# A four-layer graph network on one core: the second linear layer of the edge stages in two half products, and the loading of weights and zeros moved into the sort loop

## The chip, the cores and the metric

The kernel runs on one core of a Trainium2 chip. The metric is the time of one execution on the device in microseconds (us). Runs of one kernel agree within some 0.2%.

## What is computed

The program takes 12500 nodes with 16 features and 412500 edges (sorted by target) with 8 features and a weight, and runs four graph layers, each behind a LayerNorm and a ReLU and with a residual. The change touches the third layer, an encode-process network with 64 features, cut here to its edge part:

```python
def _mlp(x, w0, b0, w1, b1):
    return jax.nn.silu(x @ w0 + b0) @ w1 + b1
def _ln(x, g, b):
    m = jnp.mean(x, axis=-1, keepdims=True)
    v = jnp.var(x, axis=-1, keepdims=True)
    return (x - m) * jax.lax.rsqrt(v + LN_EPS) * g + b

e = _ln(_mlp(edge_feat, edge_enc_w0, edge_enc_b0, edge_enc_w1, edge_enc_b1), edge_enc_g, edge_enc_beta)
for s in range(2):
    ce = jnp.concatenate([e, n[senders], n[receivers]], axis=-1)
    e = e + _ln(_mlp(ce, edge_blk_w0[s], edge_blk_b0[s], edge_blk_w1[s], edge_blk_b1[s]), ...)
    agg = jax.ops.segment_sum(e, receivers, num_segments=num_nodes)
    ...
```

The other layers gather node features along the edges, weight them and sum them per target (or, in the first, per source).

## The kernel before

All work is in f32 but for some selection matrices. The program is one sequence of stages on one core:

1. **Start-up** (0 to 179 us). Constants; some 110 small DMAs on SyncE's queue for the weights of all layers (`load_w`, `load_b`, `pair_diag`, `bias_rows`, `twice`), with a little VectorE work on them (centering, splitting biases into three bf16 parts, block-diagonal copies); a zero tile of 128 x 6336 and ten DMAs that fill the sums in DRAM with it (`prep`, L322 to L327); LayerNorm of the nodes (`relu_ln`, L733 on) and a table for the first layer; `window_starts` (L340 to L358), which finds where the edges of each window of 128 targets begin.
2. **Sort loop** (`sort_edges`, to 4634 us). 98 windows of 128 targets. Per window `keys`, `hot_cells`, `count`, `look_up` and `rank` work out on VectorE and TensorE a row for each of 4480 records, and `scatter` (L597) writes them with 35 indirect DMAs that GpSimd issues; `s_row` (L593) is the tile of rows. Windows further back are read again and take the first layer's messages (`gather`, `products`, `message`, `to_sources`, L641 to L675). The order on TensorE, VectorE, ScalarE (ACT) and SyncE is written out by hand, window stages of lags 0 to 5 in one round, 103 rounds. The tile `s_row` has three buffers and the record tile `rec` four; a load of the next record tile waits on SyncE for an earlier window's scatters.
3. **Edge encoder** (4653 to 6786 us), **layer 2** (to 8155 us), **first edge update** (8333 to 10856 us), **second edge update** (11061 to 13350 us), with node work between them, then two GCN passes to the end.

The edge encoder and both updates run the same loop, `over_pairs`: 49 pairs of windows, ten chunks `c` of up to four blocks of 128 edges in two halves (features of two edges side by side on 128 partitions, 64 features each). The order of the engines is written out by hand; `new` is the pair whose hidden layer is made, `old` the pair before, which is normalised and summed. Per chunk: `hidden` (TensorE: first linear layer; in the updates the products L1507 and L1514 with features and gathered tables, in the encoder L1409), `scale` (VectorE: LayerNorm's factor and selection matrices), `features` (TensorE turns the old chunk, L1254, and ACT or VectorE writes it), `output` (the second linear layer, `outs`), `activate` (ACT: silu, L1209), `to_targets` (TensorE: sums per target, L1273).

`outs` (L1211 on) makes the second linear layer of a chunk: a bias product of 512 columns in bf16 (L1216), then per block of 128 edges a product of the hidden features (128 x 128, the stationary operand) with a 128 x 128 matrix that holds the 64 x 64 weights twice on its diagonal (L1218; `w1x` has them crossed, for odd chunks of the updates). All go into one PSUM bank `po`; ACT reads it twice, for the squares (L1221) and the copy `y` (L1223), and VectorE sums the squares (L1224). PSUM has eight banks here: `usual` gives two to `pt` (turns), five to `po` (hidden layers, outputs and other sums), one to `pa` (sums per target).

Other lines that are used below: `sums` of the encoder's `Adding` (L806: products of a 128 x 128 matrix with 16 columns) and the small product of a bias with weights (L278 to L280).

Of the kernel before, what the change touches and what calls it, by code (L numbers as in the profile page):

```python
# [19 lines left out]
P = 128  # L20
# [27 lines left out]
def tile_gnn(ctx: ExitStack, tc: tile.TileContext, a: dict, out: bass.AP):  # L48
# [23 lines left out]
    usual = dict(pt=2, po=5, pa=1)  # L72
    summing = dict(pt=2, po=4, pa=2)

    def bank(tag):
        pool, bufs = now[0]
        return pool.tile([P, 512], F32, name=tag, bufs=bufs[tag])
# [53 lines left out]
    def pair_diag(name, src, centered):  # L131

        d = consts.tile([P, P], F32, name=name)
        two = consts.tile([P, 64], F32, name=name + "_2")
        v.memset(d, 0.0)
        sp.dma_start(two[0:64, :], src)
        sp.dma_start(two[64:128, :], src)
        if centered:
            center(two, 64)
        v.tensor_copy(d[0:64, 0:64], two[0:64, :])  # L140
        v.tensor_copy(d[64:128, 64:128], two[64:128, :])
        return d

    def bias_rows(name, src, centered):

        b = consts.tile([3, 64], F32, name=name + "_f")
        sp.dma_start(b, row_bc(src, 64, 3))
        if centered:
            center(b, 64)
        part = consts.tile([3, 3, 64], BF16, name=name + "_p")  # L150
        back = consts.tile([3, 64], F32, name=name + "_b")
        acc = consts.tile([3, 64], F32, name=name + "_a")
        for k in range(3):
            v.tensor_copy(part[:, k, :], b)
            v.tensor_copy(back, part[:, k, :])
            v.tensor_sub(b, b, back)
            if k == 0:
                v.tensor_scalar(acc, back, ident[0:3, 0:1], None, op0=ALU.mult)
            else:
                v.scalar_tensor_tensor(acc, back, ident[0:3, k:k + 1], acc, op0=ALU.mult, op1=ALU.add)  # L160
        r = consts.tile([P, 8, 64], BF16, name=name)
        v.memset(r, 0.0)
        v.tensor_copy(r[0:3], acc[:, None, :].to_broadcast([3, 8, 64]))
        return r.rearrange("p t f -> p (t f)")
# [27 lines left out]
    wml = load_w("wml", a["L0_gnn_W_msg_lin"], 16, 16)  # L192
    v.tensor_scalar(wml, wml, 0.25, None, op0=ALU.mult)
    wupd = load_w("wupd", a["L0_gnn_W_upd_tp"].rearrange("i h k -> i (h k)"), 16, 256)
    v.tensor_scalar(wupd, wupd, 1.0 / 16.0, None, op0=ALU.mult)
    wul = load_w("wul", a["L0_gnn_W_upd_lin"], 16, 16)
    v.tensor_scalar(wul, wul, 0.25, None, op0=ALU.mult)
    w1t = load_w("w1t", a["L1_w_iao"], 16, 128)
    w1c = consts.tile([P, 16], F32, name="w1c")
    for j in range(8):  # L200
        sp.dma_start(w1c[16 * j:16 * j + 16, :], a["L1_w_iao"][:, 16 * j:16 * j + 16])
    b1_l1 = load_b("b1_l1", a["L1_gnn_bias"], 16)

    p2 = "L2_gnn_"
    ne_w0 = load_w("ne_w0", a[p2 + "node_enc_w0"], 16, 64)
    ne_b0 = load_b("ne_b0", a[p2 + "node_enc_b0"], 64)
    ne_w1 = load_w("ne_w1", a[p2 + "node_enc_w1"], 64, 64)
    center(ne_w1, 64)
    ne_b1 = load_b("ne_b1", a[p2 + "node_enc_b1"], 64)
    center(ne_b1, 64)  # L210
    ne_g = load_b("ne_g", a[p2 + "node_enc_g"], 64)
    ne_be = load_b("ne_be", a[p2 + "node_enc_beta"], 64)

    ee_w0 = consts.tile([P, 8, 64], F32, name="ee_w0")
    v.memset(ee_w0, 0.0)
    for t in range(TS):
        sp.dma_start(ee_w0[8 * t:8 * t + 8, t % 8, :], a[p2 + "edge_enc_w0"])
    ee_w0 = ee_w0.rearrange("p t f -> p (t f)")

    ec_w0 = consts.tile([P, 8, 64], F32, name="ec_w0")  # L220
    v.memset(ec_w0, 0.0)
    for t in range(8):
        sp.dma_start(ec_w0[WORDS * t:WORDS * t + 8, t, :], a[p2 + "edge_enc_w0"])
        sp.dma_start(ec_w0[WORDS * t + W_ONE:WORDS * t + W_ONE + 1, t, :], row_bc(a[p2 + "edge_enc_b0"], 64, 1))
    ec_w0 = ec_w0.rearrange("p t f -> p (t f)")
    ee_b0 = bias_rows("ee_b0", a[p2 + "edge_enc_b0"], False)
    ee_w1 = pair_diag("ee_w1", a[p2 + "edge_enc_w1"], True)
    ee_b1 = bias_rows("ee_b1", a[p2 + "edge_enc_b1"], True)
    ee_g = load_b("ee_g", a[p2 + "edge_enc_g"], 64)
    ee_be = load_b("ee_be", a[p2 + "edge_enc_beta"], 64)  # L230
# [8 lines left out]
    ee_g2 = twice("ee_g2", a[p2 + "edge_enc_g"])  # L239
    ee_be2 = twice("ee_be2", a[p2 + "edge_enc_beta"])  # L240

    eb, nb = [], []
    for s in range(2):
        w0, f = a[p2 + "edge_blk_w0"][s], {}
        f["w0e"] = pair_diag(f"eb_w0e{s}", w0[0:64, :], False)
        f["w0sd"] = consts.tile([64, 128], F32, name=f"eb_w0sd{s}")
        sp.dma_start(f["w0sd"][:, 0:64], w0[64:128, :])
        sp.dma_start(f["w0sd"][:, 64:128], w0[128:192, :])
        f["b0"] = load_b(f"eb_b0{s}", a[p2 + "edge_blk_b0"][s], 64)
        f["w1"] = pair_diag(f"eb_w1{s}", a[p2 + "edge_blk_w1"][s], True)  # L250
        f["w1x"] = consts.tile([P, P], F32, name=f"eb_w1x{s}")
        v.memset(f["w1x"], 0.0)
        sp.dma_start(f["w1x"][0:64, 64:128], f["w1"][64:128, 64:128])
        sp.dma_start(f["w1x"][64:128, 0:64], f["w1"][0:64, 0:64])
        f["b1"] = bias_rows(f"eb_b1{s}", a[p2 + "edge_blk_b1"][s], True)
        f["g"] = load_b(f"eb_g{s}", a[p2 + "edge_blk_g"][s], 64)
        f["be"] = load_b(f"eb_be{s}", a[p2 + "edge_blk_beta"][s], 64)
        f["g2"] = twice(f"eb_g2{s}", a[p2 + "edge_blk_g"][s])
        eb.append(f)
        f = {}  # L260
        f["w0"] = load_w(f"nb_w0{s}", a[p2 + "node_blk_w0"][s], 128, 64)
        f["b0"] = load_b(f"nb_b0{s}", a[p2 + "node_blk_b0"][s], 64)
        f["w1"] = load_w(f"nb_w1{s}", a[p2 + "node_blk_w1"][s], 64, 64)
        center(f["w1"], 64)
        f["b1"] = load_b(f"nb_b1{s}", a[p2 + "node_blk_b1"][s], 64)
        center(f["b1"], 64)
        f["g"] = load_b(f"nb_g{s}", a[p2 + "node_blk_g"][s], 64)
        f["be"] = load_b(f"nb_be{s}", a[p2 + "node_blk_beta"][s], 64)
        nb.append(f)

    eb[0]["sum_be"], eb[1]["sum_be"] = consts.tile([P, 64], F32, name="sum_be"), eb[1]["be"]
    v.tensor_add(eb[0]["sum_be"], eb[0]["be"], ee_be)

    be0 = twice("eb_be2", a[p2 + "edge_blk_beta"][0])
    be_w0e = consts.tile([P, 64], F32, name="be_w0e")
    with banks(**usual):
        pb0 = bank("pa")
        pe.matmul(pb0[:, 0:64], lhsT=be0[0:64, :].to_broadcast([64, P]), rhs=eb[1]["w0e"][0:64, 0:64], start=True,  # L278
                  stop=True)
        v.tensor_copy(be_w0e, pb0[:, 0:64])  # L280
    dec_w0 = load_w("dec_w0", a[p2 + "dec_w0"], 64, 64)
    dec_b0 = load_b("dec_b0", a[p2 + "dec_b0"], 64)
    dec_w1 = load_w("dec_w1", a[p2 + "dec_w1"], 64, 16)
    dec_b1 = load_b("dec_b1", a[p2 + "dec_b1"], 16)
    gw1 = load_w("gw1", a["L3_w1_t"], 16, 32)
    gb1 = load_b("gb1", a["L3_gnn_b1"], 32)
    gw2 = load_w("gw2", a["L3_w2_t"], 32, 16)
    gb2 = load_b("gb2", a["L3_gnn_b2"], 16)
# [33 lines left out]
    sp.dma_start(X, a["x"].rearrange("(p c) d -> p c d", c=C))  # L322
    with tc.tile_pool(name="prep", bufs=1) as wk:
        zero = wk.tile([P, (C + 1) * 64], F32, name="zero")
        v.memset(zero, 0.0)
        for t in [*g_l0, g_l1, *g_l2, *g_gc, t_acc]:
            sp.dma_start(t.rearrange("(p c) d -> p (c d)", p=P), zero[:, :t.shape[0] // P * t.shape[1]])  # L327
# [7 lines left out]
    def window_starts(wk):  # L335
# [4 lines left out]
        sp.dma_start(di, a["dst"].rearrange("(p j) -> p j", p=P))  # L340
        v.tensor_single_scalar(di, di, 7, op=ALU.arith_shift_right)
# [24 lines left out]
    def sort_edges():  # L366


        with tc.tile_pool(name="ws", bufs=1) as wk:
            window_starts(wk)  # L370
        with tc.tile_pool(name="so1", bufs=1) as one, tc.tile_pool(name="so", bufs=2) as ed, \
# [38 lines left out]
            with tc.manual_schedule(engines={et.PE, et.DVE, et.Activation, et.SP}):  # L410
                ws = [Window(g, k, ed) for g in range(ND)]
                ws[0].load()
                for g in range(ND + LAG):
                    def at(lag):
                        return [ws[g - lag]] if 0 <= g - lag < ND else []
# [49 lines left out]
                    for w in at(LAG - 2):  # L465
                        w.slot_rows()
            ok = one.tile([1, 1], F32, name="ok")
# [707 lines left out]
    class Pair:  # L1175
# [5 lines left out]
        def __init__(self, m, ed):  # L1181
            self.m, self.ed, self.ft, self.hot, self.ys = m, ed, {}, {}, {}
# [23 lines left out]
        def silu(self, po, c):  # L1206
            n = self.blocks(c) * P
            self.hid = self.ed.tile([P, 4 * P], F32, name="hidn", bufs=3)
            sc.activation(self.hid[:, :n], po[:, :n], AF.Silu)  # L1209

        def outs(self, c, w1, b1):  # L1211
# [593 lines left out]
```

## Time and profile before

| | us |
|---|---|
| median of 11 runs | 15569.72 (15546.02 to 15581.85) |
| profiled execution | 15571.9, of it the span of instructions 15570.1 |
| start-up to the first sort key | 179.4 |
| first scatter to last scatter of the sort | 214.3 to 4572 |
| edge encoder, 49 pairs | 4653 to 6786 |
| first, second edge update, 49 pairs each | 8333 to 10856, 11061 to 13350 |

| engine | busy us (share of the span) |
|---|---|
| TensorE, products | 11479.6 (74%) |
| TensorE, weight loads | 9472.5 (61%), beside the products |
| VectorE | 12500.1 (80%) |
| ACT | 6075.3 (39%) |
| GpSimd | 7104.4 (46%) |

The shares are means over stages with different bounds, so a stage has to be read by itself. PE is TensorE, PEld its weight loads, DVE VectorE, ACT ScalarE, POOL GpSimd, SP SyncE; a line number is one of the kernel. The durations of matmuls are partly modelled and overlap; what one costs is read from the start of one to the start of the next.

### The profile page before, as it was taken

What the parts mean: (1) busy time and instruction counts of PE and PEld (TensorE: products, weight loads), DVE (VectorE), ACT (ScalarE), POOL (GpSimd) and SP (SyncE); (2) the same over time, 40 slices, a digit from 0 to 9 for tenths busy, and PEclk for the clock granted to TensorE, in tenths of its full rate; (3) what the DMA queues carried; (4) which work ended last, traced back from release to release, by engine and by line L of the source; (5) the groups of instructions that cost most, each with busy time, mean ns of one, the idle gap of its engine ahead of it and who ended that gap; (6) DMA issues with size and microseconds to landing.
All of it is one profiled execution on the core that took longest, in us unless ns stands there. A gap on an engine that the chain in (4) does not pass through costs nothing. (4 is left out here: it accounts for less than half of the span.)

```text
span 15570.1 us, 386432 instructions
## 1 busy us (share of the span) xinstructions
PE 11479.6 (74%) x160695; PEld 9472.5 (61%) x161327; DVE 12500.1 (80%) x23622; ACT 6075.3 (39%) x10025; POOL 7104.4 (46%) x6387
## 2 busy tenths in 40 slices
PE   2555555555559999968887999998799999666565
PEld 1544544454457777758875777776577777544444
DVE  6999999999977777778886888887688888566666
ACT  0233323332335555538872333332233333244444
POOL 3777777777753333325541222221233333155455
PEclk7777777777779999989998999999899999767666
DMA  2111111111114444436664555555444444277777
GB/s 80 44 45 44 41 44 45 45 40 45 45 34 123 126 125 125 125 107 181 182 170 132 159 160 156 159 158 145 118 121 123 120 121 126 70 213 209 183 209 198
DMA packets 1361577, 1827.92 MB, mean 117 GB/s; under 512 B 501594, under 2 KB 794970, under 8 KB 1358526
## 3 DMA queue, kind: packets, MB, share of 16 engines
q1 hardware_dynamic: 1079624, 1721.34, 36.3%
q0 software_dynamic: 258720, 76.68, 4.7%
q8 instruction: 1275, 20.89, 0.5%
q10 hardware_dynamic: 21462, 4.95, 0.1%
q14 instruction: 496, 4.06, 0.1%
HBM read 1296.64 MB, written 504.92 MB: 116 GB/s over the span
## 5 line engine op out<-in xcount | busy, mean ns | idle before, releaser
L597 POOL DMA_INDIRECT cells<-rec,s_row x3430 | 3312.0, 966 | 1075.2 <-issue 1035.5
L1467 POOL DMA_INDIRECT xo<-t_src,c x980 | 1284.3, 1310 | 3847.5 <-DMA c<-cells 1563.5
L641 PE MATMUL pl<-win,hot_dt 128*128 128x128 f32 x7252 | 1363.2, 364 | 2026.2 <-DVE wide L650 1598.1
L641 PEld LDWEIGHTS pl<-win,hot_dt 128*128 128x128 f32 x7252 | 1271.9, 272 | 2096.1 <-DVE wide L650 1646.2
L1221 ACT ACTIVATE sq<-po 128x512 f32<-128x512 f32 (+1 forms) x1470 | 831.4, 566 | 3147.1 <-PE po L1218 3142.8
L1224 DVE TENSOR_REDUCE nsum<-sq 128x8 f32<-128x512 f32 (+1 forms) x1470 | 947.0, 644 | 1068.3 <-ACT sq L1221 1061.6
L1273 PE MATMUL pa<-hot,y 128*64 128x128 f32 x21756 | 1550.6, 281 | 79.1 <-DVE hot L1238 72.3
L1011 POOL DMA_INDIRECT xo<-t_gc,c x980 | 1046.1, 1067 | 1222.0 <-DMA places<-slot_lo 378.3
L1238 DVE TENSOR_TENSOR hot<-iota_row,lod 128x512 f32<-128x512 f32 x2352 | 1515.6, 686 | 0.0
L666 ACT ACTIVATE parted<-pre 32x256 f32<-32x256 f32 x784 | 324.4, 414 | 2940.4 <-DVE pre L662 2933.6
L812 POOL DMA_INDIRECT g_l<-summed,row x490 | 827.1, 1688 | 1392.3 <-ACT summed L808 1090.6
L1273 PEld LDWEIGHTS pa<-hot,y 128*64 128x64 f32 x21756 | 1181.5, 137 | 278.1 <-issue 85.7
L1082 DVE TENSOR_REDUCE x<-po 128x128 f32<-128x384 f32 x1176 | 648.9, 552 | 588.5 <-PE po L1073 538.5
L1059 ACT ACTIVATE off<-places,minus_col 98x1024 bf16<-98x1024 uint8 x784 | 897.4, 1145 | 263.6 <-DMA places<-slot_lo 218.9
L1209 ACT ACTIVATE hidn<-po 128x512 f32<-128x512 f32 (+1 forms) x1470 | 854.7, 581 | 343.8 <-PE po L1514 284.0
L1514 PE MATMUL po<-hot_dt,td 128*64 128x256 f32 (+2 forms) x7056 | 981.9, 395 | 7.6 <-DVE hot_dt L1490 7.6
L1011 POOL DMA_INDIRECT xo<-t_h,c x490 | 629.0, 1284 | 722.2 <-DMA c<-cells 269.3
L1233 DVE TENSOR_TENSOR y<-y,nr 128x512 f32<-128x512 f32 (+1 forms) x1470 | 947.7, 645 | 5.1
L1091 DVE TENSOR_TENSOR hot_d<-iota_row,c 128x1024 f32<-128x1024 f32 (+1 forms) x882 | 949.0, 1076 | 0.2 <-issue 0.2
L1514 PEld LDWEIGHTS po<-hot_st,tab 98*64 98x64 f32 x25088 | 869.7, 138 | 114.7 <-issue 1.5
L1060 ACT ACTIVATE hot_s<-off,one_col 98x1024 bf16<-98x1024 bf16 x784 | 900.2, 1148 | 25.5
L1514 PE MATMUL po<-hot_st,tab 98*64 98x64 f32 x25088 | 867.1, 222 | 0.0
(380 smaller groups left out, 25621.0 us busy)
## 6 DMA issues: line engine op xcount, KB each, us to landing
hot_dk<-keep_t SPq DMA_DIRECT2D x588, 512.0 KB
e_feat<-ft SPq DMA_DIRECT2D x882, 256.0 KB
ft<-e_feat SPq DMA_DIRECT2D x882, 256.0 KB
c<-cells SPq DMA_DIRECT2D x392, 296.0 KB
keep_t<-hot SPq DMA_DIRECT2D x392, 256.0 KB
ud<-slot_lo SPq DMA_DIRECT2D x98, 1024.0 KB
c<-cells SPq DMA_DIRECT2D x147, 592.0 KB
us<-slot_lo SPq DMA_DIRECT2D x98, 784.0 KB
```

What stands on the lines that cost most here:

```text
L597: ins = gp.indirect_dma_start(out=self.cells, out_offset=bass.IndirectOffsetOnAxis(ap=self.row[:, t:t + 1], axis=0), in_=self.rec[:, t, :] ...
L641: pe.matmul(pl[:, t * P:(t + 1) * P], lhsT=self.hots[t0 // 16][:, o:o + P], rhs=self.win, start=True, stop=True, skip_group_check=True)
L1011: gp.indirect_dma_start(out=out[:, t, :], out_offset=None, in_=table, in_offset=bass.IndirectOffsetOnAxis(ap=c[:, TC + t, W_SRC:W_SRC + 1] ...
L1059: sc.activation(off, u, AF.Abs, bias=minus_col[:C, :])
L1060: sc.activation(o, off, AF.Relu, bias=one_col[:C, :], scale=-1.0)
L1091: v.tensor_tensor(o[:, :k, :], bc_mid(iota_row, k), bc_last(self.c[:, t0:t0 + k, W_LD], P), ALU.is_equal)
L1224: return lambda: v.tensor_reduce(self.sums[:, 8 * c:8 * c + 2 * k], sq[:, :2 * k, :], AX.X, ALU.add)
L1233: v.tensor_tensor(w, w, bc_last(self.r[:, 8 * c:8 * c + 2 * k], 64), ALU.mult)
L1238: v.tensor_tensor(hot[:, w].rearrange("p (h t) d -> p h t d", h=2), iota_row[:, None, None, :].to_broadcast([P, 2, 2, P]), lo[:, :, :, Non ...
L1273: pe.matmul(self.acc[64 * w:64 * w + 64, 0:P], lhsT=lhsT, rhs=rhs, start=c == 0 and i < 2, stop=c == 9 and i >= len(work) - 2, skip_group_ ...
L1467: gp.indirect_dma_start(out=self.xo[:, w, t, :], out_offset=None, in_=t_src[s], in_offset=bass.IndirectOffsetOnAxis(ap=self.c[:, w, TC + t ...
L1514: pe.matmul(out[o:o + 64], lhsT=lhsT, rhs=rhs, start=start, stop=stop, skip_group_check=True)
```

## The change

It has two parts. The weights, their preparation and the zeros are no longer loaded ahead of the sort: a generator `weights(zero)` issues them in some 77 small steps, one at the top of each round of the sort loop from the second round on; the zero tile has 1666 columns in place of 6336 and fills the sums in 17 DMAs; `window_starts` comes first, ahead of LayerNorm and the first table, and the small product of a bias with weights comes behind the loop. And `outs` makes two bias products of 256 columns and two products for each block, one on array rows 0 to 63 and one on rows 64 to 127 (128 weight columns and 64 moving columns each), whose sums go to two PSUM banks of a new tile `pw`, of which there is one; `po` has three banks in place of five. In `over_pairs` the silu of a chunk comes ahead of the output of the chunk before.

```diff
-    usual = dict(pt=2, po=5, pa=1)
+    usual = dict(pt=2, po=3, pa=1, pw=1)
...
-        return pool.tile([P, 512], F32, name=tag, bufs=bufs[tag])
+        return pool.tile([P, 2, 512] if tag == "pw" else [P, 512], F32, name=tag, bufs=bufs[tag])
...
-    wml = load_w("wml", a["L0_gnn_W_msg_lin"], 16, 16)
...
-    ee_b1 = bias_rows("ee_b1", a[p2 + "edge_enc_b1"], True)
...
+    def weights(zero):
+        ee_w0 = consts.tile([P, 8, 64], F32, name="ee_w0")
+        v.memset(ee_w0, 0.0)
+        yield
...
+        n = zero.shape[1]
+        for t in [*g_l0, g_l1, *g_l2, *g_gc, t_acc]:
+            w = t.shape[0] // P * t.shape[1]
+            for o in range(0, w, n):
+                k = min(n, w - o)
+                sp.dma_start(t.rearrange("(p c) d -> p (c d)", p=P)[:, o:o + k], zero[:, :k])
+                yield
+        for name, (d, two, centered) in diags.items():
+            if centered:
+                center(two, 64)
+                yield
+            v.tensor_copy(d[0:64, 0:64], two[0:64, :])
+            v.tensor_copy(d[64:128, 64:128], two[64:128, :])
+            yield
...
-        zero = wk.tile([P, (C + 1) * 64], F32, name="zero")
-        v.memset(zero, 0.0)
-        for t in [*g_l0, g_l1, *g_l2, *g_gc, t_acc]:
-            sp.dma_start(t.rearrange("(p c) d -> p (c d)", p=P), zero[:, :t.shape[0] // P * t.shape[1]])
...
+                zero = one.tile([P, C * 17], F32, name="zero")
+                v.memset(zero, 0.0)
+                others = weights(zero)
                 for g in range(ND + LAG):
+                    if g:
+                        next(others, None)
...
+                for _ in others:
+                    pass
...
-        def outs(self, c, w1, b1):
-            k, po, hid = self.blocks(c), bank("po"), self.hid
-            n = k * P
-            pe.matmul(po[:, :n], lhsT=ones_r, rhs=b1[:, :n], start=True, stop=False, skip_group_check=True)
+        def outs(self, c, w1, b1, swapped=0):
+            k, pw, hid = self.blocks(c), bank("pw"), self.hid[c]
+            for half in range(2):
+                pe.matmul(pw[:, half, :k * 64], lhsT=ones_r, rhs=b1[:, :k * 64], start=True, stop=False,
+                          skip_group_check=True)
             for j in range(k):
-                pe.matmul(po[:, j * P:(j + 1) * P], lhsT=hid[:, j * P:(j + 1) * P], rhs=w1, start=False,
-                          stop=j == k - 1, skip_group_check=True)
+                for h in range(2):
+                    x, half = slice(64 * h, 64 * h + 64), h ^ swapped
+                    pe.matmul(pw[:, half, j * 64:(j + 1) * 64], lhsT=hid[x, j * P:(j + 1) * P],
+                              rhs=w1[x, 64 * half:64 * half + 64], start=False, stop=j == k - 1, skip_group_check=True)
+            out = pw[:, :, :k * 64].rearrange("p h (j f) -> p j h f", f=64)
             sq = self.ed.tile([P, 8, 64], F32, name="sq")
-            sc.activation(flat(sq)[:, :n], po[:, :n], AF.Square)
+            sc.activation(sq[:, :2 * k, :].rearrange("p (j h) f -> p j h f", h=2), out, AF.Square)
             self.ys[c] = self.ed.tile([P, 4, P], F32, name="y", bufs=12)
-            sc.copy(flat(self.ys[c])[:, :n], po[:, :n])
+            sc.copy(self.ys[c][:, :k, :].rearrange("p j (h f) -> p j h f", h=2), out)
...
+                    if new and c < 10:
+                        new.activate(c)
                     if new and c:
                         reduce = new.output(c - 1)
-                    if new and c < 10:
-                        new.activate(c)
...
-    def sort_edges():
-        with tc.tile_pool(name="ws", bufs=1) as wk:
-            window_starts(wk)
...
+    with tc.tile_pool(name="ws", bufs=1) as wk:
+        window_starts(wk)
     with tc.tile_pool(name="n0", bufs=1) as wk:
         relu_ln(H, X, wk)
...
+    with banks(**usual):
+        pb0 = bank("pa")
+        pe.matmul(pb0[:, 0:64], lhsT=be0[0:64, :].to_broadcast([64, P]), rhs=eb[1]["w0e"][0:64, 0:64], start=True,
+                  stop=True)
+        v.tensor_copy(be_w0e, pb0[:, 0:64])
```

## The prediction

> **What bounds the kernel now.** I read the page first (its table of 40 slices shows stages with different bounds), then the busy times by stretch, the start-up on VectorE, who waits for whom in the sort loop, and last TensorE's order of time around the second linear layer.
>
> ```profile
> core 0: us, PE busy (x) PEld busy (x) DVE busy (x) ACT busy (x) POOL busy (x), PEclk, DMA share, GB/s
> 2000.00:2250.00 250.00, 135.31 (x996) 128.12 (x997) 228.20 (x385) 70.63 (x89) 190.24 (x197) 0.71 0.14 41
> 5000.00:5250.00 250.00, 234.10 (x2268) 184.27 (x2292) 186.74 (x413) 144.44 (x276) 103.26 (x60) 1.00 0.45 124
> 9000.00:9250.00 250.00, 239.15 (x3205) 187.55 (x3226) 216.85 (x408) 76.59 (x160) 59.27 (x50) 0.99 0.53 159
> ```
>
> Columns: stretch, length, busy time of each engine, granted clock, DMA. In the edge encoder (4653 to 6786 us) and the two updates (8333 to 10856, 11061 to 13350) TensorE is busy 94 to 96% at full clock: there TensorE's time is the stage's time. The sort loop (first row) is another matter: VectorE 91%, GpSimd 76%.
>
> ```profile
> 55.16 0.23 DVE L280 COPY be_w0e<-pa 128x64 f32<-128x64 f32 x1 [2.66 <-PE pa L278]
> 92.68 1.79 DVE L733 TENSOR_REDUCE ln_s<-X 128x98 f32<-128x1568 f32 x1 [37.29 <-DMA t_acc<-zero]
> 144.20 1.84 DVE L341 TENSOR_SCALAR ws_di<-ws_di 128x3232 int32<-128x3232 int32 x1 [6.51 <-DMA ws_di<-in_dst]
> 179.36 0.19 DVE L502 CAST s_src<-rec 128x35 f32<-128x35 int32 x1 [0.36 <-DMA rec<-in_rec]
> ```
>
> VectorE's order of time (start, length, instruction, idle before it). Weights fill the first 55 us, the zero fills another 37, and the sort's first key is made only at 179.36.
>
> ```profile
> L597 POOL DMA_INDIRECT cells<-rec,s_row x3430: 954/958/1442, 214.3 to 4570.9; - x191
>   issue: 1035.5, 3396
> L593 DVE TENSOR_SCALAR s_row<-s_inc x98: 182/182/282, 213.8 to 4496.7; 128x35 int32<-128x35 f32 x98
> ```
>
> The sort's scatters and the row numbers that they take from VectorE. GpSimd issues 3430 scatters back to back, 1.27 us each (0.96 and 0.30 of issue), from 214.3 to the end of the loop: 35 x 1.27 = 44.4 us a window. VectorE's last row number is ready at 4496.9; the last window's scatters start 35 x 1.27 before 4572, at about 4528. So GpSimd sets the loop, and VectorE is 31 us ahead at its end.
>
> **Part 1, weights and zeros into the loop.** Removed ahead of the loop: some 120 DMA issues on SyncE, the zero fill and the 37 us behind it, and some 115 VectorE instructions. What stays runs in a new order: window starts, LayerNorm, table, sort. By the old rows: the load of the target indices, issued at 1.3 instead of 137.6, lets L341 start after the same 6.6 us, at 8; from there to the end of the window starts 29.1 (144.2 to 173.3), so 37; LayerNorm and table 43.3 (92.7 to 136.0), so 80.5; the wait for the table's stores 1.5, so 82; the loop's constants 5.8 (173.5 to 179.4) and the smaller zero tile 1.4 (6336 columns took 5.34 us, 1666 are left), so 89.5 for the first key. With the 0.48 us memset now ahead of the first scatter: **89 us earlier**.
>
> What moves into the loop costs VectorE 22 to 25 us (those 115 instructions, by their own rows in the start-up), in 47 or so of 103 rounds. Cover: the 31 us of lead. The lead does not shrink smoothly: it fell from 41.7 us to 31.1 in steps of about 1.27, GpSimd's period, and GpSimd itself ran at 44.7 instead of 44.4 a window after such a step. If each of the 47 rounds loses a whole step, 60 us are lost, 29 more than the lead, and 77 disturbed windows at 0.3 make 23. So 0 to 52 us; I take 10, near the lower end, because plain busy time fits under the lead. A gain is excluded: no scatter leaves.
> On SyncE the added DMAs stand behind the loads of a round and ahead of the next record load, which waits some 40 us per round for scatters: that wait hides them, the 17 zero fills (0.85 MB each) too. Without it, some 130 issues at 0.4 to 0.6 us would be 65 us. The small bias product between sort and encoder adds one product and one copy (2.7 and 0.2 us before): 2 us. Three instead of five `po` banks cost nothing I can see: between stages VectorE's takes are what TensorE waits for.
>
> **Part 2, the second linear layer.** 49 pairs x 10 chunks x 3 stages = 1470 calls.
>
> ```profile
> 4627.30 2.91 PE L675 MATMUL acc<-parted,hot_s 128*98 128x64 f32 x32
> ...
> 5003.73 1.29 PE L806 MATMUL po<-over,same 128*128 128x16 f32 x10
> 5004.95 1.08 PE L1409 MATMUL po<-eatt,ec_w 128*64 128x256 f32 x8
> ...
> 5006.46 0.38 PE L1216 MATMUL po<-ee_b,ones_r 128*128 128x512 bf16 x1
> 5006.68 1.05 PE L1218 MATMUL po<-ee_w,hidn 128*128 128x128 f32 x8
> 5007.66 0.55 PE L1273 MATMUL pa<-hot,y 128*64 128x128 f32 x6
> ...
> 9506.68 1.09 PE L1507 MATMUL po<-ft,eb_w0e 64*64 64x512 f32 x8
> 9507.70 1.08 PE L1514 MATMUL po<-hot_dt,td 128*64 128x256 f32 x8
> 9508.61 1.10 PE L1514 MATMUL po<-hot_st,tab 98*64 98x64 f32 x32
> 9509.65 0.66 PE L1254 MATMUL pt<-ident,y 128*128 128x128 f32 x4
> ```
>
> TensorE in order of time; "128*64" is the tile of stationary rows and columns, then the moving data, then the number of records (an f32 product is two). The next line's start gives the cost. A call before: bias 0.22, eight records and the turn to the next tile shape 0.98, together 1.20 us (5006.46 to 5007.66).
> Do the two halves run side by side? L1507 says yes: eight quarter-array records of 512 columns take 1.02 us, 0.51 for each four, though two of the four share columns and differ in rows only.
> Does that make them shorter? After the change each half has 64 rows but still 128 weight columns, and only 64 moving columns. L806 is the nearest row: 128 weight columns, 16 moving ones. Ten records take 1.22 us; less the turn (about 0.2), nine gaps of 0.112, the same as L1218 with 128 moving columns. L675 with 98 weight columns and 64 moving ones runs at 0.086 (2.91 less 0.25 for the last one's way through, over 31), L1514 with 64 weight columns at 0.059 a pair (1.04 less 0.1, over 16). So a step costs what its weight columns cost, and eight steps of 0.112 remain: the halved stream saves nothing.
> The Trainium skill (TensorEngine Tiling (Array Packing), Theoretical Speedup) gives up to 2x for a contraction of 64 or less; by that, eight steps of 0.056 would take 0.45 us off each call and the sum below would end near 15050. Its page TensorE: Matmul & The Clock Gate, LDWEIGHTS (loading the stationary operand), makes the load time go by columns and not by rows, which speaks against this change; no row here has a load of 64 rows by 128 columns.
> What is added: one more change of tile shape, between the bias (128 rows) and the halves. Such a change costs 0.09 (L1218 to L1273 0.205 instead of 0.112), and the first weights can't load ahead: 0.02 (L806's first gap 0.133) to 0.11 (a whole load); the last step may end 0.04 sooner. Together +0.10 to +0.20, I take 0.13: 1470 x 0.13 = 191. TensorE's waits in these stages (4 to 6%) swallow a little: **+181 us** (bounds 130 to 290).
> The swap of the silu and the output frees ACT's silu from waiting for the product; TensorE waited for it 8 to 20 us in stretches of 1500 to 2000 us: taken as 0, at most 40 us gained in all three. The outputs now have one buffer, so a call's bias waits for the last call's copy. ACT ends that 1.4 us after the last product (0.3, 0.5 and 0.6); TensorE has at least the 1.05 us of L1273, a turn and usually the next hidden layer before it needs the buffer, so 0; at a pair's last chunk up to 0.4 x 147 = 60 us. If ACT read two banks more slowly (0.6 us each now) it would bind more often.
>
> **Sum.** Profiled execution 15571.9 (span 15570.1 and 1.8 around it): -89 +10 +2 +181 = 15676. The median of the runs is 2 us lower: **15674**.
>
> **Rivals.**
> (1) The load isn't the floor with 64 rows: a step costs what L1514's pair does, 0.059. 8 x 0.053 saved, 0.15 for the change of shape: -0.27 a call, x 1470 x 0.95 = -377, with part 1's -77: 15116. It decides wherever a step falls below 0.095. For it: quarter products overlap in L1507. Against: L806. 15%.
> (2) The change of shape costs nothing (the bias drains under the loads, the swap of the silu pays): only part 1 is left, -77: 15493. 12%.
> (3) One output buffer or a slower two-bank read binds: 0.07 to 0.15 more per call, 15780 to 15890. Against: ACT is 30 to 58% busy there. 12%.
> (4) The halves' loads run one after the other: eight more loads of 0.112 and 0.13, about 1.03 x 1470: 17010. Against: L1507's four loads. 5%.
> (5) That part 1 does not pay, because the loop's end is set elsewhere, is against the back-to-back scatters; a starved loop (+42) lies inside the range.
> My own sum: 56%, its own range 15600 to 15770.
>
> **Numbers.** The range 15470 to 15890 holds the sum's case, (2) and (3). A measurement of this kernel can tell about 0.2% (31 us) from no change. Faster: (1), (2): 0.28. Same: 0.07, the lower edge of the sum. Slower: 0.65.
>
> **What would show it.** First scatter near 125 us; 44.4 us a window kept, VectorE's last row number still ahead of GpSimd's use of it; from the bias to `to_targets` near 1.33 us a call, in steps of 0.112; the encoder longer than its 43.5 us a pair (2133 over 49) by about 1.2. Steps of 0.06, or an encoder below 43.5 us a pair, make it wrong; waits of the bias products for ACT show (3); a first scatter much later than 125 us, or GpSimd waiting for row numbers, makes part 1 wrong.

## The result and the profile after

The changed kernel takes 15709.3 us (median of 8 runs, 15687.43 to 15739.93) against 15574.03 us before (30 runs): a ratio of 1.009, 95% interval [1.0081, 1.0098], 135 us more. The profiled execution after took 15732.1 us (its span is 15730.3), 160 more than the one before and 23 above the median of its own runs. Where the 160 us are, from the two traces (a stage lasts from its first silu to the end of its last one; the tail from the last scatter's end to the encoder's first silu):

| us | before | after | difference |
|---|---|---|---|
| first scatter | 214.3 | 122.3 | -92.0 |
| first scatter to the end of the last | 4357.6 | 4378.5 | +20.9 |
| tail | 83.7 | 110.6 | +26.9 |
| encoder | 2098.8 | 2151.8 | +53.0 |
| update 1 | 2491.7 | 2572.5 | +80.8 |
| update 2 | 2262.8 | 2327.1 | +64.3 |
| all between and behind | | | +6.2 |

The busy times by stretch of the changed kernel (stretch, length, then PE, PEld, DVE, ACT, POOL, granted clock, DMA):

```profile
2000.00:2250.00 250.00, 128.02 (x915) 121.08 (x916) 227.84 (x412) 68.06 (x84) 190.26 (x197) 0.69 0.14 41
5000.00:5250.00 250.00, 236.29 (x2707) 180.72 (x2705) 183.14 (x397) 138.88 (x263) 99.33 (x55) 1.00 0.46 126
9000.00:9250.00 250.00, 240.41 (x3364) 182.21 (x3362) 204.62 (x388) 74.78 (x148) 56.79 (x48) 0.93 0.50 151
```

TensorE still sets the encoder and the updates (94 to 96% busy), and VectorE has become less busy there: it has the same work in a longer time. The third row has a clock of 0.93.

The scatters and the row numbers of the changed kernel, with what GpSimd sat idle for (us, times):

```profile
L635 POOL DMA_INDIRECT cells<-rec,s_row x3430: 952/958/1444, 122.3 to 4499.8; - x191
  issue: 1029.3, 3376
...
  DVE s_row L631: 14.0, 9
...
L631 DVE TENSOR_SCALAR s_row<-s_inc x98: 182/183/283, 121.8 to 4455.9; 128x35 int32<-128x35 f32 x98
```

The first scatter starts at 122.3, where about 125 was forecast. But nine times GpSimd now waits for a row number, which never happened before: the last one is ready at 4456.1, only 0.8 us ahead of its first scatter (31.1 before). The prediction had named this, GpSimd waiting for row numbers, as a sign that its part 1 is wrong.

TensorE behind the last scatter (it ends at 4500.8), and SyncE's first load of the encoder:

```profile
4526.25 10.52 PE L713 MATMUL acc<-parted,hot_s 128*98 128x64 f32 x64
4557.00 10.54 PE L713 MATMUL acc<-parted,hot_s 128*98 128x64 f32 x64
4583.65 6.13 PE L713 MATMUL acc<-parted,hot_s 128*98 128x64 f32 x64
```
```profile
4603.10 0.39 SPq L1225 DMA_DIRECT2D c<-cells  x1
```

Each of the three lines closes a round's messages, 27 to 31 us apart. The kernel before had two such rounds left behind its last scatter. That third round is what the lost lead costs here. Its price is not fixed, though: the run mix (below) ends with the same 0.8 us of lead and the same three rounds, but they are 21 to 24 us apart, and its tail is 95.4 us instead of 110.6. A stretch of one round's length of the changed kernel and one of mix, with granted clocks of 0.61 and 0.86:

```profile
4530.00:4560.00 30.00, 24.67 (x138) 23.37 (x137) 14.25 (x14) 12.57 (x15) 0.00 (x0) 0.61 0.08 25
4523.00:4547.00 24.00, 17.91 (x140) 16.55 (x138) 14.67 (x14) 13.23 (x18) 0.00 (x0) 0.86 0.10 31
```

The second linear layer in the encoder, TensorE in order of time:

```profile
5005.32 0.66 PE L1296 MATMUL pt<-ident,y 128*128 128x128 f32 x4
5005.81 0.38 PE L1254 MATMUL pw<-ee_b,ones_r 128*128 128x256 bf16 x2
5006.12 1.11 PE L1259 MATMUL pw<-ee_w,hidn 64*128 64x64 f32 x16
5007.16 1.09 PE L1315 MATMUL pa<-hot,y 128*64 128x128 f32 x16
```

From the bias (5005.81) to `to_targets` (5007.16) it is 1.35 us, against 1.20 before. Record by record: a pair of halves starts every 0.112 us, exactly as a whole product did (0.111); the first pair follows the second bias by 0.202, and the second pair the first by 0.160. Two halves run side by side and gain nothing, and a change of tile shape with an unhidden first load comes on top.

Who TensorE waited for in update 2 after the change (us, times, longest):

```profile
PE pa L1315 <- DVE hot L1280: 60.0, 49, 1.3
PE po L1556 <- DVE hot_dt L1532: 8.7, 48, 0.5
PE pw L1254 <- ACT y L1265: 1.8, 2, 1.2
```

The single buffer `pw` is waited for twice in 490 calls (in update 1 twice as well, 1.8 us, in the encoder 7 times, 2.8 us): rival (3) is out.

### The profile page after: what moved, and what is told of

It reads as the page before. It is cut to its first block, busy times and chain, and to the rows that moved or that the text cites. A ratio compares the mean times of both kernels' runs of the same rounds, so it can differ in the third digit from the quotient of the medians.

```text
span 15730.3 us, 411243 instructions
## 1 busy us (share of the span) xinstructions
PE 11802.1 (75%) x173674; PEld 9568.5 (61%) x173675; DVE 12502.3 (79%) x23622; ACT 6158.3 (39%) x10025; POOL 7183.4 (46%) x6387
## 5 line engine op out<-in xcount | busy, mean ns | idle before, releaser
L850 POOL DMA_INDIRECT g_l<-summed,row x490 | 885.8, 1808 | 1417.7 <-ACT summed L846 1092.2
L1263 ACT ACTIVATE sq<-pw 128x512 f32<-128x512 f32 (+1 forms) x1470 | 831.6, 566 | 1103.8 <-PE pw L1259 1077.9
```

## The experiments

They came in four sessions on four chips, and in three of them the kernel before took 19315, 19095 and 19350 us instead of 15570: there TensorE and ScalarE waited for their own instructions in the sort loop (shown at the end), a window took some 72 us instead of 44.5, and VectorE's lead was 0.3 us in nearly all windows (11 at most, in the first). Only the last session (swap, mix; before 15557.77 us) is like the one of the prediction. Every ratio below is against before on the same chip in the same session. What concerns the lead in the sort loop can be read in the last session alone; the encoder, which had hardly any such waits, can be read in all with the old layer (2094 to 2099 us everywhere) and with halves (2149 to 2152), but not with four products: the same code took 2006 to 2013 us in the first three and 1948 in the last.

**part1**: the change without `pw`, halves and swap.

```diff
-    usual = dict(pt=2, po=3, pa=1, pw=1)
+    usual = dict(pt=2, po=5, pa=1)
...
-                    if new and c < 10:
-                        new.activate(c)
                     if new and c:
                         reduce = new.output(c - 1)
+                    if new and c < 10:
+                        new.activate(c)
```

> Part 1 alone (weights, zeros and window starts as in the change; second layer, order of silu and output and banks as before). Theory A, VectorE's lead is spent: the first scatter stays 92 us earlier, the loop pays 21 us of starved scatters and 27 us of a longer tail after the last scatter, so 15570 - 44 = about 15526, with the lead near 0.5 us at window 97. Rival B, the prediction's own sum (plain busy time hides under the lead): 15493, and the 48 us are due to part 2.

Measured: 19269.5 us, ratio 0.9975 [0.996, 0.999], 45 us less. The first scatter comes at 123.3 and the last ends at 7141.3, against 213.4 and 7184.4 in part2, which has the old loop: of 90 us the loop gives back 47. The sum is A's, but on that chip there was no lead to lose, so A's mechanism isn't shown by it; B's -77, a ratio of 0.996, lies just at the edge of the interval.

**part2**: before with halves, two banks and swap, and the old start-up.

> Part 2 alone (halves, two banks, swapped order; start-up as before). Theory A, the change of tile shape and its unhidden load: 0.150 us a call x 1470 = 220, of which about 22 are swallowed by waits that the swap removes: 15570 + 198 = about 15768, steps of a pair at 0.105. Rival B, a good part of the trace's +198 is a lower granted clock in the updates and not the products: then the three stages cost 53 each, 15729.

Measured: 1.0129 [1.0112, 1.0147], 241 us more. Against part1 (old layer, same chip) the encoder is 54.5 longer (2151.9), update 1 106 (3023.4), update 2 46 (2498.5). The encoder repeats the change's own +53. A's size (+198) is nearer than B's (+159), but both lie below the interval (216 to 284), and B's cause is there as well: in update 1 the granted clock is 0.89 against 0.93 in part1, while the waits that the view puts down to TensorE's own instructions are fewer there (172 us against 215).

**quad**: part 2 with four products of 64 rows x 64 columns.

```diff
-                pe.matmul(pw[:, half, :k * 64], lhsT=ones_r, rhs=b1[:, :k * 64], start=True, stop=False,
+                    pe.matmul(pw[y, h ^ swapped, :k * 64], lhsT=ones_r[x, y], rhs=b1[x, :k * 64], start=True, stop=False,
...
-                    pe.matmul(pw[:, half, j * 64:(j + 1) * 64], lhsT=hid[x, j * P:(j + 1) * P],
+                        pe.matmul(pw[y, half, j * 64:(j + 1) * 64], lhsT=hid[x, j * P + 64 * q:j * P + 64 * q + 64],
```

> Part 2 with each half split once more by columns: four products of 64 rows x 64 columns side by side, the bias too in that shape (ones and bias rows also at partitions 64 to 66). Theory A, a step costs what its weight columns cost: 0.056 to 0.059 for the four, so seven steps save 0.34 us and one bias pass 0.11, two more costs of shape change are paid as in part 2: about 0.97 us a call instead of 1.20, 1470 x 0.95 x 0.23 = 320 less: about 15250. Rival B, the records count and not the columns (0.029 us each, as the pair at 0.0585 suggests): four make 0.117, no gain in the steps: 15620 to 15700. Rival C, VectorE (83 to 88% busy in the updates) takes over as the bound: half of A's gain, 15410.

Measured: 0.9889 [0.9871, 0.9907], 211 us less. TensorE in the encoder of quad, in order of time:

```profile
8008.55 0.30 PE L1220 MATMUL pw<-ee_b,ones_r 64*64 64x256 bf16 x4
8008.68 0.63 PE L1226 MATMUL pw<-ee_w,hidn 64*64 64x64 f32 x32
8009.24 1.09 PE L1283 MATMUL pa<-hot,y 128*64 128x128 f32 x16
```

A call is 0.70 us (8008.55 to 8009.24) and a step of four products 0.0585: half the weight columns, half the step. Rival B (0.117) is refuted, and so is the reading that a step's cost lies in the number of records. With the change's own 0.112 for 64 rows and 128 columns this settles what the step costs: its weight columns, whatever the rows. The whole gained less than A's 320 because the gain met new waits: the encoder fell by 85 only (2012.7 against part1's 2097.4, and some 25 of the 85 belong to the swap, see below), as TensorE then waited for VectorE's `key` and `y` (C in part), and update 2 grew by 30, where TensorE waited 322 times for its own instructions, more than for VectorE's one-hots:

```profile
PE pw L1226 <- issue: 166.1, 322, 1.2
PE pa L1283 <- DVE hot L1248: 88.8, 48, 1.9
```

Such waits are 169 us in all there, some 101 in part1's update 2. But the granted clock of update 2 is lower as well, 0.91 against 0.97. Which of the two made the stage longer, and whether one made the other, is not shown.

**late**, and **late2**, the same kernel on another chip: part1, but the weights' VectorE work behind the loop in the program.

```diff
+        yield "rest"
         for name, (d, two, centered) in diags.items():
...
-                for _ in others:
-                    pass
...
                 sp.dma_start(t_acc.rearrange("(s q) f -> q s f", q=C), got)
+            for _ in others:
+                pass
```

> Part 1 with the loads, memsets and zeros in the loop, but the weights' other VectorE work (centring, copies, three-part biases) after the loop instead of in its rounds 41 to 77; second layer as before. Theory A, each round with such work costs VectorE a step of its lead: the lead stays near 38 us less the 11 us that it lost before anyway, the loop ends 86 to 92 us earlier, and the work itself (about 20 us) falls into VectorE's idle time before the encoder's first load lands: 15480 to 15505. Rival B, it is the DMA issues on SyncE that hold the loop up: as part 1 alone, 15526.

> The late kernel once more, for the case that this chip gives TensorE its instructions without the gaps of 0.3 to 2.5 us that the last one showed. Theory A, lost lead: -85 to -92 against before on the same chip, the lead in the middle of the loop near 38 us, the tail after the last scatter as before (76 us). Rival B, the DMA issues cost the lead: about -45.

Measured: 0.9941 [0.9922, 0.9961] and 0.9932 [0.9916, 0.9949], 95 and 124 us less. Both expectations miss what the kernel did. Outside the hand-ordered loop the order is the scheduler's, and it put the work not behind the loop but at its front, as VectorE's order of time in mix (the same loop) shows, between two instructions of the second window's ranks:

```profile
171.49 0.22 DVE L131 TENSOR_REDUCE row_mean<-ee_w 128x1 f32<-128x64 f32 x1 [24.29 <-DMA ee_w<-in_L_gnn_edge_enc_w]
171.63 0.49 DVE L601 TENSOR_TENSOR s_eq<-s_eq,before 128x324 f32<-128x324 f32 x1
```

So late is a variant "early", and the DMA issues were not cleared or convicted by it. The trace of the changed kernel says more on rival B: from window 12 to window 23 (counted from 0) SyncE issues 74 of the weights' loads, and the lead goes from 38.9 to 38.8 us, so these cost nothing. From window 28 to 40, with 11 of the 17 zero fills and no work of the weights on VectorE, it falls from 38.8 to 33.6, where it stays as it is in before and swap; the first six zero fills cost nothing, so this is open. In late's session the loop ended 47 us sooner than that of part1; what late does to the lead is read below, in mix.

**best**, and **best2**, the same kernel on another chip: late and quad together.

> The late kernel (start-up loads in the loop, the weights' VectorE work after it) together with the quad kernel's second layer. Theory A: both gains add: -85 to -92 from the start-up and, where TensorE gets its instructions without gaps, a call of 0.70 us instead of 1.20 and one more change of shape ahead of it (0.09): 0.41 x 1470 = 600 if TensorE alone set the stages; waits for VectorE's y and keys, which the encoder of the quad run showed as new, leave about half: -300. In all about -390 against before on the same chip. Rival B, instructions: where TensorE waits for issue, four products for one eat the gain in the updates and the sum is near -94 - 211 = -305.

> The combination of late and quad once more, on whatever chip comes. Theory A: where TensorE gets its instructions without gaps, the loop ends 86 to 92 us earlier than before with a lead of some 25 to 38 us near its end and the tail after the last scatter as before (76 us), the encoder takes 2005 us instead of 2099, and both updates gain as well (150 to 230 each): about 15570 - 500 = 15070. Where it waits for issue, as on the last two chips: about 360 less than before, update 2 longer than before by 90. Rival B: update 2 gains nothing on any chip, since VectorE's one-hots (hot) end its waits, and then 15570 - 90 - 94 - 200 = 15190.

Measured: 0.9807 [0.979, 0.9823] and 0.9815 [0.9798, 0.9831], 356 and 365 us less. Encoder 2005.6 and 2010.9, update 2 2474.7 and 2479.2: the gain of update 2 is missing where TensorE waits for instructions, as quad had it (the granted clock of update 2 is 0.91 in all three runs, 0.99 in tiny with the old layer). The first sum lies between what the two theories gave; the 360 that the second text gave for such a chip, worked out from the first run, came.

**tiny**: before with one more VectorE instruction in each of 70 rounds.

```diff
+                    if 20 <= g < 90:
+                        v.memset(tiny, 0.0)
```

> The kernel before with one more VectorE instruction (a fill of 8 numbers of one row, some 0.06 us) in each of 70 rounds of the sort loop, 20 to 89. Theory A, VectorE is tied to the period of GpSimd's scatters (1.27 us) and an added instruction costs a whole step or nothing, by where it falls: the lead of 41 us falls by up to 70 x 1.27 = 89, so it runs out and the time grows by 40 to 60. Rival B, plain busy time: 70 x 0.06 = 4 us of lead, no change of the time beyond 10.

Measured: 1.0001 [0.999, 1.0011]. It tells nothing of A: on that chip GpSimd waited for VectorE in every window (lead 0.3 us in nearly all), so nothing was tied to the scatters' period.

**bias64**: part 2 with the bias products in the halves' shape.

```diff
-            for half in range(2):
-                pe.matmul(pw[:, half, :k * 64], lhsT=ones_r, rhs=b1[:, :k * 64], start=True, stop=False,
+            for h in range(2):
+                x = slice(64 * h, 64 * h + 64)
+                pe.matmul(pw[:, h ^ swapped, :k * 64], lhsT=ones_r[x, :], rhs=b1[x, :k * 64], start=True, stop=False,
```

> Part 2 alone, but the two bias products in the shape of the halves (64 rows x 128 columns, one in each, side by side). Theory A, what part 2 lost is the change of shape between the bias and the halves with its unhidden load: the change moves ahead of the bias (0.203 instead of 0.109), the two biases take one pass (0.12), the first gap loses its 0.05, eight steps of 0.105 stay: 0.203 + 0.12 + 0.74 + 0.20 = 1.27 from the transposes to the next shape, against 1.31 before and 1.46 in part 2: 0.04 x 1470 = 60 less than before. Rival B, the halves themselves cost more than whole products: between before and part 2, +100 to +200.

Measured: 1.0069 [1.0052, 1.0086], 113 us more, against A's -60. TensorE in its encoder:

```profile
8005.96 0.66 PE L1261 MATMUL pt<-ident,y 128*128 128x128 f32 x4
8006.55 0.28 PE L1219 MATMUL pw<-ee_b,ones_r 64*128 64x256 bf16 x2
8006.67 1.00 PE L1224 MATMUL pw<-ee_w,hidn 64*128 64x64 f32 x16
8007.60 1.09 PE L1280 MATMUL pa<-hot,y 128*64 128x128 f32 x16
```

From the last transpose to `to_targets` it is 0.205 + 1.053 = 1.26 us, as A had it, against 0.109 + 1.200 before and 0.109 + 1.350 after the change; the encoder is 76.5 us shorter than part2's (2075.4 against 2151.9), where 0.2 us a call would make 98. So A holds for the call: the bias in the full shape cost the change its 0.2 us. But the halves gain nothing by it: swap (below), with whole products and the same order of silu and output, has an encoder of 2073.8, so the 19 us by which tiny's is longer (2094.4, old order) are the swap's, and the 490 x 0.05 = 25 that the calls should save are not seen in the stage. The whole got slower in the updates (+70 and +54 against tiny), and its +113 lies in B's range. Waits for instructions don't explain it in update 1: the view has 171 us of them, against 195 in tiny. The granted clock is lower, 0.89 and 0.95 in the two updates against 0.93 and 0.99; what lowers it is not shown.

**after2**: the change on a chip of the third session.

> The change itself beside before on the same chip. Where TensorE gets its instructions without gaps: +135 to +160, as found. Theory A for a chip where it waits for issue: the parts add as measured on such a chip, -45 and +241: about +195, a ratio of 1.010. Rival B: the parts share a wait there, and the sum is off by more than 40.

Measured: 1.0081 [1.0059, 1.0104], 151 us more. The sum of part1 and part2 (1.0104) lies at the edge of the interval: B is not excluded, but the parts add within what can be measured.

**swap**: before with the silu of a chunk ahead of the output of the chunk before it, and nothing else.

```diff
+                    if new and c < 10:
+                        new.activate(c)
                     if new and c:
                         reduce = new.output(c - 1)
-                    if new and c < 10:
-                        new.activate(c)
```

> The kernel before with one thing of part 2 alone: the silu of the next chunk ahead of the output of the last, on ScalarE and TensorE. Theory A: the swap takes away waits of the products for the silu (a call before spends 0.238 us on average from bias to first product in the encoder where 0.216 is the least), and that is what keeps the encoder at +53 us instead of 490 x 0.15 = 73: the encoder 10 to 20 us shorter than before (2094 to 2099), the whole 20 to 50 less. Rival B: the swap does nothing alone, and the encoder's waits hide the difference elsewhere: encoder within 5 us of before.

Measured: 15472.95 against 15557.77 us, 0.9951 [0.9935, 0.9968], 85 us less, more than A had. Encoder 2073.8 (-25.0), update 1 2468.6 (-23.1), update 2 2233.5 (-29.3), each against the trace of before in the prediction's session. Who TensorE waited for in update 2 of the kernel before:

```profile
PE pa L1273 <- DVE hot L1238: 65.7, 47, 1.4
PE po L1218 <- issue: 23.5, 148, 0.2
PE po L1218 <- ACT hidn L1209: 8.2, 48, 0.8
```

and of swap:

```profile
PE pa L1273 <- DVE hot L1238: 66.5, 49, 1.4
PE po L1514 <- DVE hot_dt L1490: 7.6, 47, 0.2
```

The 8.2 us put down to the silu are gone, and with them the 23.5 of small gaps of up to 0.2 us ahead of the same products that the view calls "issue": 31.7 in all, where the stage lost 29.3. In the encoder and update 1 the view has only 4.5 and 2.5 us of such waits, although these stages gained as much. Read from start to start, the time from the last product ahead of the layer to the layer's last product is 17 and 21 us shorter there in sum: gaps that the view does not list.

**mix**: best, with whole products and one bias in update 2.

```diff
+                if s == 1:
+                    return self.whole(c, f["w1x"] if c % 2 else f["w1"], f["b1"])
```

> The combination (late loads, four products of 64 x 64) in the encoder and update 1, whole products of 128 x 128 with one bias in update 2. Theory A, instructions: on chips where TensorE waits for issue, update 2 lost 90 us to them with four times the products, so whole products bring it back to 2380 to 2450, and the whole is some 450 less than before: a ratio of 0.977. Rival B: update 2 is bound by VectorE's one-hots in either form and loses by something else in the new order (the reads of two banks): then it stays near 2475 and the ratio at 0.981.

Measured: 15202.89 against 15557.77 us, 0.9774 [0.9758, 0.979], 355 us less: the fastest version here. It fell into the ordinary session, so A against B on update 2 stays untested: it takes 2230.7, as in swap. That the ratio is the 0.977 of A is luck, since A gave it for a chip on which TensorE waits for issue. The stages of mix, encoder and update 1:

```profile
4593.00:6541.00 1948.00, 1773.45 (x31368) 1321.77 (x31368) 1556.01 (x3414) 1141.30 (x2281) 770.05 (x477) 1.00 0.50 134
```
```profile
8127.00:10493.00 2366.00, 2261.05 (x44290) 1641.53 (x44288) 2138.28 (x4046) 794.18 (x1560) 596.53 (x482) 0.97 0.57 165
```

Beyond swap the four products save 125 us in the encoder (1948.3) and 102 in update 1 (2366.4), where the calls alone would give 490 x (0.503 - 0.094) = 200 each (0.503 a call less, one more change of shape): VectorE is at 80% and 90%, and TensorE waits 114 us for its `key` in the encoder (68 before). In its loop the first scatter is at 121.8, the last ends at 4498.1, the tail is 95.4: 62 us of the start-up's 92 stay (59 against swap on the same chip), against 44 in the change. The weights' 23.3 us of VectorE work in rounds 0 to 12, and 29 us of waits for their DMAs, starve one window by 13.9 us and leave a lead of 14.7 us at window 12 where swap has 41.3. It goes on falling, to 0.8 at the end (swap: 34.9), though only three later windows have work of the weights; why is open.

## Why the prediction was right, and where it was not

Forecast +104 us on the profiled execution, measured +160 (median +135); inside the range, on the side that was given 65%. By its terms:

**The start-up**, -89: measured -92.0.

**The loop**, +10 and +2 for the small product: measured +20.9 and +26.9, 47.8 together (the product's own 2 us are not seen: from the store of the sums to the encoder's first load it is 12.5 us, 12.9 before). This is the step that failed: "I take 10, near the lower end, because plain busy time fits under the lead". Two things were wrong in it. First, the busy time isn't the price. VectorE's row numbers of windows 28, 40 and 77, before and after:

```profile
1424.70 0.18 DVE L593 TENSOR_SCALAR s_row<-s_inc 128x35 int32<-128x35 f32 x1 [0.21 <-DMA cells<-rec,s_row]
1957.19 0.18 DVE L593 TENSOR_SCALAR s_row<-s_inc 128x35 int32<-128x35 f32 x1 [0.21 <-DMA cells<-rec,s_row]
3605.81 0.18 DVE L593 TENSOR_SCALAR s_row<-s_inc 128x35 int32<-128x35 f32 x1 [0.21 <-DVE s_inc L591]
```
```profile
1329.37 0.18 DVE L631 TENSOR_SCALAR s_row<-s_inc 128x35 int32<-128x35 f32 x1 [0.21 <-DMA cells<-rec,s_row]
1870.32 0.18 DVE L631 TENSOR_SCALAR s_row<-s_inc 128x35 int32<-128x35 f32 x1 [0.21 <-DVE s_inc L629]
3564.80 0.18 DVE L631 TENSOR_SCALAR s_row<-s_inc 128x35 int32<-128x35 f32 x1 [0.21 <-DVE s_inc L629]
```

Over all these windows 54.3 us more pass than before (2235.4 instead of 2181.1). 8.5 of them fall up to window 40, where VectorE has no work of the weights (see late). From 40 to 77 it has 102 instructions of the weights in 35 of the rounds, 22.0 us busy, and loses 45.9 (1694.5 instead of 1648.6): 1.31 us for each such round. That is the other bound of the prediction, a step of 1.27 lost in each round; that the loss comes in such steps is argued from the sum and not shown. Second, the lead is not a reserve to be spent: VectorE's rounds behind the last scatter have to be done too, and what the lead loses comes back there as a third round. The lead fell from 31.1 to 0.8 us, and the tail grew by 26.9 (in mix, with a higher clock in the tail, by 11.7 for the same 0.8). The sum counted only what would go beyond the lead; the whole loss was to be counted.

**The second linear layer**, +181: measured +198.1, by errors that cancel, which is luck. (a) The steps: "eight steps of 0.112 remain" is exact. (b) The change of shape: 0.13 a call was taken, 0.150 measured: 0.095 for the change (0.311 from bias to first product instead of 0.216) and 0.05 for the unhidden load; x 1470 = 220. (c) The swap was "taken as 0, at most 40 us gained": swap alone gave 77 in the three stages. The prediction took the waits for the silu alone from its view; in update 2 small gaps of 0.2 us at the same products stood under "issue", and in the other two stages in hardly any row. (d) The granted clock: 0.97 and 0.99 in the updates after the change, 0.98 and 1.00 before; 0.01 of some 2570 and 2330 us is about 50 together, an estimate; the clock records of the traces, summed over the three stages, give the same (60 us lost before, 110 after). 220 - 77 + 50 = 193. But by the same records 19 of swap's 77 us are clock as well (41 lost), so without counting them twice it is 212, and some 14 us stay open. In the encoder, at full clock before, after and in swap, it closes without (d): 490 x 0.150 - 25.0 = 48.5, measured 53.0. What moved the clock is not shown; with halves it is lower in update 1 in all four runs (0.97, 0.89, 0.89, 0.88) than with whole products in the same sessions (0.98, 0.93 and 0.93; none was traced beside the last).

**The rivals**: (1) needed a step below 0.095; it is 0.112. The doubling that the Trainium skill (TensorEngine Tiling (Array Packing), Theoretical Speedup) gives as the most for short contractions did not come for halves of 64 rows; it came (0.0585) when the weights had 64 columns as well. Its rule that load time goes by columns and not by rows (TensorE: Matmul & The Clock Gate, LDWEIGHTS (loading the stationary operand)), for which the prediction had no row of 64 by 128, agrees: a step of these halves takes 0.112. (2) failed, since the change of shape costs 0.15, though the swap that it also named pays 77. (3) failed: 1.8 us. (4) failed: pairs run side by side. (5) half came true: the start-up pays, and the loop gave back half of it.

## What to carry to other kernels

Before work moves into a loop that "has time", ask what its lead is worth behind the last iteration: lead that is spent is paid at the end, and small instructions in a loop tied to another engine cost here twice their busy time (45.9 us for 22.0). Splitting a product by rows of the array frees nothing while the weight columns set the step; split the columns too, and keep the bias in the same tile shape, since each change of shape cost 0.1 to 0.15 us here; and read the granted clock of each stage beside its waits. Of a change with several parts run each alone: here the smallest one, an order of two calls, was a gain of 0.5% hidden in a loss.

## What the hardware did that I had not expected

In three of the four sessions TensorE went without instructions in the sort loop. Its order of time in part1, with the idle time ahead of each:

```profile
2058.72 0.27 PE L565 MATMUL po<-s_ohs,ones_bf 128*128 128x128 bf16 x1 [2.44 <-issue]
2061.51 0.37 PE L679 MATMUL pl<-win,hot_dt 128*128 128x128 f32 x1 [2.52 <-issue]
2064.32 0.37 PE L679 MATMUL pl<-win,hot_dt 128*128 128x128 f32 x1 [2.44 <-issue]
```

One product every 2.8 us, though nothing that the profile shows holds it; of the 3000 us from 1000 on, 955 are such gaps of over 0.2 us, nearly all between 20 and 50 us after the start of a window's scatters, which take 44. GpSimd then waits for the row numbers in turn:

```profile
POOL cells L635 <- DVE s_row L631: 113.5, 4, 28.8
```

The kernel was 23 to 24% slower for it, before and after the change alike, and the traces of the ordinary session have no such gap in these stretches. Why a session has them is open. Open is also why a round with more VectorE work lost 1.31 us for 0.63 us of it: tiny was made for this and met such a session.
